# A Mamba-and-experts block on one Trainium2 core: order of the experts' products, the gate and a LayerNorm step inside a scan's slots

## The chip, the cores and the metric

The kernel runs on one core of one Trainium2 chip, as one launch. The metric is the device time of that core in microseconds, the median of three runs. A core has a matrix engine (PE, with its weight loads shown as PEld), a vector engine (DVE), an activation engine (ACT), a general engine (POOL) and a queue that starts the transfers (SP). Each works through its own list in order and waits on the others where the program says so.

## What is computed

The input is two images of 256 channels by 64x64 positions, read as two sequences of 4096 tokens. In short:

```python
x = x + conv_mamba(group_norm(x))                     # layer 0, inner width 256
t = tokens(x)
n = layer_norm(t)
t = t + mamba_fwd(ln(n)) + flip(mamba_bwd(flip(ln(n)))) + n   # layer 1, inner width 512 each
n = layer_norm(t)
w = softmax(mean_over_batch(n) @ Wr + br)             # 8 weights per token position
h = relu(bn(n @ W1[e]));  h = relu(bn(h @ W2[e]));  y_e = h @ Wo[e] + bo[e]
t = t + sum_e w[:, e] * y_e

# a mamba, for each channel d and state s (16 states), over time:
h = exp(dt * A[d, s]) * h + dt * B[s] * x
y[d] = sum_s C[s] * h[d, s] + D[d] * x;   out = (y * silu(z)) @ W_out
```

All of it is fp32.

## The kernel before

**The scan part.** Six Mamba jobs (batch 0: layer 0, forward, backward; then batch 1 the same) are each cut in 8 chunks of 512 tokens. A tile of 128 channels has 16 states, and the recurrence of 32 channels by 4 states fits 128 partitions, so a chunk is worked in groups of 4 x 512 columns: 640 groups `g` for the whole kernel, four to a tile of channels, eight to a pair of tiles (`n` is the place of the group among these eight). Each group is done in two halves `h`, each a *slot*; there are 1280 slots. One slot on each engine, in the order of the loop at the end of the scan part:

- PE: the products that a plan put in the slot (`pe`: input projections L434, convolution L472, dt L521, output L771 and L773, norms), then sums over states at some slots (`emit_sum`, L735, after the table `SUMS`), then the experts' products (`pe2`, L922).
- ACT: the copy of the last state (L724, L726), the two decays `exp(dt*A)` of the *next* slot (`emit_decay`, L684, with the join of L695), then whatever the plan put in `act`.
- DVE: what the plan put in `dve0` (convolution's second step L486 and the gate's sigmoid part L563), the scan (L705), what it put in `dve` (L533, the norms L399 and L400), then the multiplication by C (`emit_times_c`, L714). In three of eight groups (`POOL_C`) that last step is POOL's (L730), and the DVE's slot is then the scan alone.
- POOL: `b = x*dt*B` (L674), its share of the C products, `xdt` (L537) and the norm's residual add (L403).

The order on every engine is fixed by hand here (`in_order`). Work for later chunks is put into slots by fixed offsets relative to the chunk's first slot `s0` (`norm`, `prepare`, `finish`): for a layer-1 chunk the gate's projection z stands at s0-6, -5, -3 and -2 (`SLOTS`), with a load of ACT's function table at s0-6. Of the forward job's LayerNorm the divide (L399, L400) and POOL's add stand at s0-39, the affine step (L407, two activations) at s0-37, the store at s0-36. The add reads the tile `nx` that the affine step then overwrites. Since chunks are 32 slots apart, s0-38 of one chunk is s0-6 of the chunk ahead of it.

**The experts inside the scan part.** When the backward job has finished a chunk of tokens, the eight experts could be applied to it. `experts()` walks over the slots and adds groups of experts' products where a running balance of PE work (`behind`), of ACT work (`act_behind`) and the three PSUM banks of `psp` (`fits`) allow. One group is two matmuls of 128x512 for one half of one layer; a pair (one expert on one chunk of one batch) has six groups and leaves its result `u` in DRAM. At most one group goes into a slot. 68 of the 128 pairs are done this way: all 64 of batch 0, and experts 0 to 3 of chunk 7 of batch 1.

**The last part.** After the scans, `load`, `route` and `layer` go over the chunks 7, 6, ..., 0. For each expert not done early: L1162 twice with a ReLU (L1166), a multiplication by the routing weight (DVE, L1207) and L1212 into a PSUM accumulator of four banks (`ym`). For each pair done early, its `u` is loaded and added (`add_early`: DVE L1193 and L1197). At the end of a chunk the DVE reads the accumulator (L1224) before the next chunk's bias product (L1183) may write it. A chunk whose pairs are all early for both batches would be placed second (`whole`, `chunks[1:1]`); before the change there is none. A scheduler orders the instructions of this part.

Of the kernel before, what the change touches and what calls it, by code (L numbers as in the profile page):

```python
# [49 lines left out]
KC = C // P  # L50
# [30 lines left out]
PE_ROOM, PE_BEHIND = 3.8, 2.5  # L81
# [48 lines left out]
def hybrid_kernel(ctx: ExitStack, tc: tile.TileContext, a: dict, out: bass.AP):  # L130
# [75 lines left out]
    with ExitStack() as st:  # L206
# [129 lines left out]
        def norm(i):  # L336

            (job, c), ck, tag, s0 = steps[i], cks[i], tags[i], starts[i]
            s = job.cols(c)
            b = job.batch  # L340

            def alloc():
                ck["nx"] = wk.tile([P, KC, T], F32, tag="nx", name=f"nx_{tag}", bufs=2)

            if job.flip:
                def load():
                    alloc()
                    nc.sync.dma_start(ck["nx"], n2_dram[b][:, NCH - 1 - c, :, :])
                sl.put(s0 - 44, "sp", load)
                return  # L350

            def load_x():
                ck["x"] = wk.tile([P, KC, T], F32, tag="x", name=f"x_{tag}")
                src = t_dram[b] if job.layer else a["x"][b].rearrange("(k p) l -> p k l", p=P)
                nc.sync.dma_start(ck["x"], src[:, :, s])

            if job.layer == 0:
                def scale():
                    alloc()
                    for k in range(KC):  # L360
                        nc.scalar.activation(
                            ck["nx"][:, k, :], ck["x"][:, k, :], AF.Identity,
                            bias=job.gb[:, k : k + 1], scale=job.gs[:, k : k + 1],
                        )
                sl.put(s0 - 32, "sp", load_x)
                sl.put(s0 - 25, "act", scale)
                return

            def mean():
                ck["ps"] = psp.tile([P, T], F32, tag="ps", name=f"mean_{tag}")
                for k in range(KC):
                    nc.tensor.matmul(
                        ck["ps"], mean_w, ck["x"][:, k, :], start=(k == 0), stop=(k == KC - 1)
                    )

            def centre():
                ck["cen"] = wk.tile([P, KC, T], F32, tag="cen", name=f"cen_{tag}")
                nc.vector.tensor_tensor(ck["cen"], ck["x"], over_channels(ck["ps"]), ALU.subtract)  # L380

            def square():
                alloc()
                nc.scalar.activation(ck["nx"], ck["cen"], AF.Square)

            def variance():
                ck["var"] = psp.tile([P, T], F32, tag="ps", name=f"var_{tag}")
                for k in range(KC):
                    nc.tensor.matmul(
                        ck["var"], mean_w, ck["nx"][:, k, :], start=(k == 0), stop=(k == KC - 1)  # L390
                    )

            def roots():
                ck["r1"] = psp.tile([P, T], F32, tag="ps", name=f"r1_{tag}")
                rsqrt(ck["r1"], ck["var"], eps5)
                rsqrt(ck["var"], ck["var"], eps10, scale=1.0 + 1e-5)

            def divide():
                nc.vector.tensor_tensor(ck["nx"], ck["cen"], over_channels(ck["r1"]), ALU.mult)  # L399
                nc.vector.tensor_tensor(ck["cen"], ck["cen"], over_channels(ck["var"]), ALU.mult)  # L400

            def add():
                nc.gpsimd.tensor_tensor(ck["x"], ck["x"], ck["nx"], ALU.add)  # L403

            def affine():
                for k in range(KC):
                    nc.scalar.activation(  # L407
                        ck["nx"][:, k, :], ck["cen"][:, k, :], AF.Identity,
                        bias=lngb[:, 1, k : k + 1], scale=lngb[:, 0, k : k + 1],
                    )  # L410

            def store():
                nc.sync.dma_start(n2_dram[b][:, c, :, :], ck["nx"])
                nc.sync.dma_start(t_dram[b][:, :, s], ck["x"])

            for d, queue, fn in (
                (-48, "sp", load_x), (-44, "pe", mean), (-43, "dve", centre), (-42, "act", square),
                (-41, "pe", variance), (-40, "act", roots), (-39, "dve", divide), (-39, "pool", add),
                (-37, "act", affine), (-36, "sp", store),
            ):  # L420

                sl.put(s0 + d + (6 if c == 0 else 0), queue, fn)
            s0 += 6 if c == 0 else 0
            sl.count(s0 - 44, 2, 0, (1,))
            sl.count(s0 - 43, 0, 1)
            sl.count(s0 - 41, 2, 4, (2,))
            sl.count(s0 - 40, 0, 0, (1,))
            sl.count(s0 - 38, 0, 2)

        def in_proj(job, ck, half, j, name):  # L430
            ps = psp.tile([P, T], F32, tag="ps", name=name)
# [8 lines left out]
        def prepare(i):  # L440
# [109 lines left out]
            def gate(j):  # L550

                v = {}

                def pe():
                    v["ps"] = in_proj(job, ck, 1, j, f"z_{tag}_{j}")

                def act():
                    v["th"] = wk.tile([P, T], F32, tag="th", name=f"thz_{tag}_{j}", bufs=3)
                    nc.scalar.activation(v["th"], v["ps"], AF.Tanh, scale=0.5)

                def dve():
                    ck["sz", j] = wk.tile([P, T], F32, tag="sz", name=f"sz_{tag}_{j}", bufs=8)
                    nc.vector.scalar_tensor_tensor(  # L563
                        ck["sz", j], v["th"], 1.0, v["ps"], ALU.add, ALU.mult
                    )

                return (0, "pe", pe), (1, "act", act), (2, "dve0", dve)

            def put(slot, work):
                for d, queue, fn in work:  # L570
# [5 lines left out]
            for j in range(nj):  # L576
                put(at["xs"][j], xs(j))
                sl.count(s0 + at["xs"][j], 2, 1, (1,))
                put(at["dt"][j], softplus(j))
                sl.count(s0 + at["dt"][j], 1, 3, (2,))  # L580
                sl.count(s0 + at["z"][j], 2, 1, (1,))
            for jp in range(nj // 2):
                put(at["conv"][jp], conv(jp))
                sl.count(s0 + at["conv"][jp], 5, 1, (1, 2))
# [271 lines left out]
        def experts():  # L856
# [4 lines left out]
            def fits(slot):  # L861

                at = sum(b[0] <= slot for b in banks)
                both = banks[:at] + [(slot, slot + 1, 0)] + banks[at:]
                return all(
                    both[k - 3][1] + both[k][2] <= both[k][0] for k in range(max(3, at - 2), min(len(both), at + 4))
                    if at in range(k - 3, k + 1)
                )
# [9 lines left out]
            def follows(l):  # L878

                k, m = divmod(len(times[l]), KC)  # L880
                if k == len(todo):
                    return None
                waits = [(l - 1, k * KC + 1, 2)] if l else []
                if m:
                    waits.append((l, k * KC, 1))
                elif k:

                    waits.append((l, k * KC - 1, 6 if l == 0 and todo[k][-1] == 0 else 5))
                    if l < 2:
                        waits.append((l + 1, k * KC - 1, 0))  # L890
                if any(n >= len(times[w]) for w, n, _ in waits):
                    return None
                return max([todo[k][0] + 3] + [times[w][n] + d for w, n, d in waits])

            for slot in range(last):
                behind = max(0.0, behind) + sl.products.get(slot, 0) + sums_in(slot) - PE_ROOM
                act_behind = max(0.0, act_behind) + sl.acts.get(slot + 1, 0) - ACT_ROOM
                if behind + 2 > PE_BEHIND or act_behind + 1.3 > ACT_BEHIND or not fits(slot):
                    continue
                for l in (2, 1, 0):  # L900
                    at = follows(l)
                    if at is None or slot < at:
                        continue
                    banks.insert(sum(b[0] <= slot for b in banks), (slot, slot + 1, 0))
                    times[l].append(slot)
                    behind += 2
                    act_behind += 1 if l == 2 else 1.3
                    break
            put = [
                (*item[1:], [times[l][k * KC + m] for l in range(3) for m in range(KC)])  # L910
                for k, item in enumerate(todo) if (k + 1) * KC <= len(times[2])
# [109 lines left out]
        for g in range(nq):  # L1021
            i, jp, n = quads[g]
            for h in range(2):
# [3 lines left out]

                if (n, h) in ((1, 0), (5, 0)) and done:
                    emit_gate(*done.pop(0))

                if (n, h) in ((1, 1), (5, 1)):
                    emit_skip(i, 2 * jp + n // SG)
                sl.run(slot, "pe")
                for m in SUMS.get((n, h), ()):
                    if g - n + m >= 0:
                        emit_sum(g - n + m)
                sl.run(slot, "pe2")
                if (n, h) in ((0, 0), (4, 0)) and g:
                    done.append(at(g - 1)[:2])

# [292 lines left out]
```

## Time and profile before

| What | us |
|---|---|
| runs | 5367.55, 5373.43, 5375.16 |
| median | 5373.43 |
| profiled execution: its own time | 5375.72 |
| profiled execution: span from first to last instruction | 5373.7 |
| first scan starts, last scan ends | 61.1, 4567.2 |
| last part | 4571 to 5374 |
| busy in the span: PE, PEld, DVE, ACT, POOL | 4432.3, 1501.3, 4634.7, 3704.5, 4191.8 |

The profile shows one execution. A group row names line, engine, operation, out<-in and count, then busy time, the mean of one instruction in ns, the engine's idle time just before them and what ended it. A row of the waits says which line waited for which, for how long in total, how often, and the longest. In a timeline, the first column is the start, the second the duration of a merged run of equal instructions, and the bracket is the idle time ahead of it. A 128x512 fp32 matmul of the program stands in the trace as two records.

### The profile page before, as it was taken

To read this page: it belongs to the slowest core of one execution; us is meant where nothing else is said; L and a number is where in the kernel's file an instruction comes from. 1 tells how busy PE (TensorE), PEld (TensorE's weight loads), DVE (VectorE), ACT (ScalarE), POOL (GpSimd) and SP (SyncE) were. 2 spreads that over 40 slices of the span, in tenths; PEclk is the share of its full clock that TensorE was granted. 3 is DMA by queue.
4 is the path that set the end of the run, shared out by engine and by line. 5 is a ranking of instruction groups with operands and counts; after the bars stand their busy time and mean duration, and the time that the engine had idled before them with its cause. 6 is when DMAs were issued, how large, how long until landed. Compare 5 with 4: busy or idle time off the path is not lost.

```text
span 5373.7 us, 47307 instructions
## 1 busy us (share of the span) xinstructions
PE 4432.3 (82%) x14920; PEld 1501.3 (28%) x14920; DVE 4634.7 (86%) x3118; ACT 3704.5 (69%) x7722; POOL 4191.8 (78%) x1062
## 2 busy tenths in 40 slices
PE   5677777676678888889888888889898987699999
PEld 1122222221222333222222322223233332243433
DVE  6998999999999999989999999999999999423222
ACT  5677677777677777888887788887877787122222
POOL 6898999999999999988899999999999998000000
PEclk8888888888888999999999999999999999799999
DMA  4455333443345554455554445445544443623211
GB/s 170 145 176 172 137 126 129 154 149 133 128 142 185 170 165 152 167 191 191 193 184 160 165 173 177 164 166 169 192 160 161 157 165 126 235 74 113 95 63 47
DMA packets 307563, 822.41 MB, mean 153 GB/s; under 512 B 34472, under 2 KB 96688, under 8 KB 265328
## 3 DMA queue, kind: packets, MB, share of 16 engines
q1 hardware_dynamic: 307312, 819.39, 44.6%
q8 instruction: 118, 1.93, 0.1%
q14 instruction: 133, 1.09, 0.1%
HBM read 638.26 MB, written 181.01 MB: 152 GB/s over the span
## 4 chain that ended last, share of the span: by engine, by line
DVE 35%; PE 26%; ACT 12%; issue 7%; POOL 4%; DMA 3%; SPq 0%; DVEq 0%; POOLq 0%; ACTq 0%
DVE da L705 17%; PE hp L1162 7%; DVE bq L714 7%; DVE bq L705 6%; ACT da L684 4%; PE ym L1212 4%; PE e L922 4%; POOL bq L674 3%; PE y L735 3%; PE conv L472 2%; PE xs L434 2%; PE o L773 1%; POOL bq L730 1%; PE dbc L501 1%; DVE sz L563 1%
## 5 line engine op out<-in xcount | busy, mean ns | idle before, releaser
L674 POOL TENSOR_TENSOR bq<-rxdt,bc 128x2048 f32<-128x2048 f32 x640 | 2892.2, 4542 | 43.5 <-issue 22.3
L684 ACT ACTIVATE da<-rdt,w_a 128x512 f32<-128x512 f32 x2560 | 1756.6, 686 | 90.2 <-DVE bq L705 44.1
L705 DVE TENSOR_TENSOR_SCAN da<-da,h_state,bq 128x1024 f32<-128x1024 f32 x700 | 1644.2, 2349 | 16.9 <-issue 7.5
L730 POOL TENSOR_TENSOR bq<-bq,bc 128x2048 f32<-128x2048 f32 x240 | 1086.5, 4527 | 275.4 <-ACT h_state L726 261.7
L735 PE MATMUL y<-bq,stack 128*32 128x512 f32 x5120 | 835.1, 676 | 345.3 <-POOL bq L730 221.4
L714 DVE TENSOR_TENSOR bq<-da,bc 128x1024 f32<-128x1024 f32 x800 | 978.6, 1223 | 24.1
L705 DVE TENSOR_TENSOR_SCAN bq<-da,h_state,bq 128x1024 f32<-128x1024 f32 x420 | 965.5, 2335 | 24.7 <-ACT da L684 24.5
L724 ACT COPY h_state<-da 128x2 f32<-128x2 f32 x799 | 125.7, 157 | 770.1 <-DVE bq L714 768.8
L922 PE MATMUL e<-eh,ew 128*128 128x512 f32 x1088 | 552.2, 635 | 66.3 <-DVE sp L533 24.7
L1166 ACT ACTIVATE h<-hp,of,sc 128x512 f32<-128x512 f32 x240 | 186.5, 777 | 467.4 <-PE hp L1162 467.4
L1207 DVE TENSOR_TENSOR h<-h,wb 128x1024 f32<-128x1024 f32 x60 | 73.5, 1225 | 426.8 <-ACT h L1166 409.3
L695 ACT ACTIVATE bq<-h_state,bq,a 128x1 f32<-128x1 f32 x1120 | 432.2, 386 | 0.1
L735 PEld LDWEIGHTS y<-bq,stack 128*32 128x32 f32 x5120 | 150.4, 116 | 970.9 <-issue 367.5
L434 PE MATMUL z<-nx,w_in 128*128 128x512 f32 x640 | 326.3, 639 | 47.9 <-DVE sp L533 29.2
L434 PE MATMUL xs<-nx,w_in 128*128 128x512 f32 x640 | 334.5, 657 | 36.6 <-DVE xc L486 29.3
L472 PE MATMUL conv<-xs,w_conv 64*64 64x512 f32 x2560 | 330.2, 622 | 4.3 <-ACT eh L933 2.4
L922 PEld LDWEIGHTS e<-eh,ew 128*128 128x128 f32 x1088 | 198.4, 196 | 414.9 <-issue 230.6
L773 PE MATMUL o<-sz,w_out 128*128 128x512 f32 x640 | 303.5, 614 | 0.8 <-DVE sz L754 0.8
L922 PE MATMUL e<-en,ew 128*128 128x512 f32 x544 | 265.0, 614 | 22.3 <-DVE fcen L821 11.8
L521 PE MATMUL dt<-dbc,w_dt 64*128 64x512 f32 x320 | 200.9, 713 | 53.6 <-ACT dbc L508 32.3
L742 PE MATMUL y<-xc,w_d 128*128 128x512 f32 x320 | 185.3, 663 | 64.2 <-DVE sz L754 64.2
L1212 PE MATMUL ym<-h,Wo 128*128 128x512 f32 x480 | 231.8, 628 | 7.0 <-DVE h L1207 7.0
(139 smaller groups left out, 5178.5 us busy)
## 6 DMA issues: line engine op xcount, KB each, us to landing
rxdt<-xdtd SPq DMA_DIRECT2D x160, 1024.0 KB, 6.0
rdt<-dtd SPq DMA_DIRECT2D x160, 1024.0 KB, 5.8
bc<-bcd SPq DMA_DIRECT2D x384, 256.0 KB, 3.1
dtd<-sp SPq DMA_DIRECT2D x160, 256.0 KB, 3.8
xdtd<-xdt SPq DMA_DIRECT2D x160, 256.0 KB, 2.9
ew<-in_W SPq DMA_DIRECT2D x136, 256.0 KB, 4.0
u<-eu SPq DMA_DIRECT2D x68, 512.0 KB, 4.0
u<-u SPq DMA_DIRECT2D x68, 512.0 KB, 3.6
```

The costliest lines, as they stand in the source:

```text
L434: nc.tensor.matmul(ps, job.w["in", half][:, k, j * P : (j + 1) * P], rhs, start=(k == 0), stop=(k == KC - 1),)
L472: nc.tensor.matmul(v[r][64 * col : 64 * col + 64, :], job.w["conv"][rows, 2 * jp + j, k, :], ck["xs", jp][rows, j, k : k + T] if k < 4 els ...
L674: nc.gpsimd.tensor_tensor(bq[g], ck["rxdt", j], over_groups(ck["bc", 0, sg]), ALU.mult)
L684: nc.scalar.activation(da[g, h][:, k, :], cks[i]["rdt", j][:, q, :], AF.Exp, scale=steps[i][0].w["a"][:, j, q * SG + sg : q * SG + sg + 1],)
L695: nc.scalar.activation(bq[g][:, q, 0:1], job.h[:, j, sg, q : q + 1], AF.Identity, scale=cks[i]["a0", j][:, h, sg : sg + 1], bias=bq[g][:, ...
L705: nc.vector.tensor_tensor_scan(b if quads[g][2] in POOL_C else d, d, b, job.h[:, j, sg, 2 * h : 2 * h + 1] if c else 0.0, ALU.mult, ALU.add,)
L714: nc.vector.tensor_tensor(bq[g][:, two, :], d, cks[i]["bc", 1, sg].rearrange("p (o t) -> p o t", o=1).to_broadcast([P, 2, T]), ALU.mult,)
L730: nc.gpsimd.tensor_tensor(bq[g], bq[g], over_groups(cks[i]["bc", 1, sg]), ALU.mult)
L735: nc.tensor.matmul(y[i, j][q * CG : (q + 1) * CG, :], stack, bq[g][:, q, :], start=False, stop=(sg == SG - 1),)
L922: nc.tensor.matmul(ps, ew[l][:, k, m * P : (m + 1) * P], key[x][:, k, :], start=(k == 0), stop=(k == KC - 1),)
L1162: nc.tensor.matmul(ps, w[:, k, m * P : (m + 1) * P], x[:, k, :], start=(k == 0), stop=(k == KC - 1),)
L1212: nc.tensor.matmul(y[:, b, m, :], we["Wo", e][:, k, m * P : (m + 1) * P], h2[b][:, k, :], start=False, stop=(e == E - 1 and k == KC - 1),)
```

## The change

Five edits, all in how work is ordered:

1. `pe2` (experts' products) runs ahead of the sums over states in a slot, not behind them.
2. The planner of the experts may put two groups into a slot: it goes over the layers (2, 1, 1, 0, 0) and checks room before each; the second half of a layer may follow the first in the same slot (wait 0 in place of 1).
3. The gate's sigmoid part (L563) moves from the queue `dve0` to `dve`, from ahead of the scan to behind it, and the planner counts its PSUM bank for two slots.
4. The affine step of the LayerNorm moves from s0-37 to s0-38, and the plan's count of it with it.
5. With this the planner places 444 groups in 74 pairs, before 408 in 68. The six more are experts 4 to 7 of chunk 7 of batch 1 and experts 0 and 1 of chunk 6. Chunk 7 is then whole, so the last part runs the chunks 6, 7, 5, 4, ..., 0, with 6, 0, 8, 8, 8, 8, 8, 8 pairs of products. In the built program 66 slots hold two groups: 27 of them at place 15 of the 16 slots of a pair of tiles, 12 each at places 9 and 3, the other 15 elsewhere; 82 groups stand ahead of sums.

```diff
             for d, queue, fn in (
...
-                (-37, "act", affine), (-36, "sp", store),
+                (-38, "act", affine), (-36, "sp", store),
...
-            sl.count(s0 - 38, 0, 2)
+            sl.count(s0 - 39, 0, 2)
...
-                return (0, "pe", pe), (1, "act", act), (2, "dve0", dve)
+                return (0, "pe", pe), (1, "act", act), (2, "dve", dve)
...
-                sl.count(s0 + at["z"][j], 2, 1, (1,))
+                sl.count(s0 + at["z"][j], 2, 1, (2,))
...
                 if m:
-                    waits.append((l, k * KC, 1))
+                    waits.append((l, k * KC, 0))
...
-                if behind + 2 > PE_BEHIND or act_behind + 1.3 > ACT_BEHIND or not fits(slot):
-                    continue
-                for l in (2, 1, 0):
+                for l in (2, 1, 1, 0, 0):
                     at = follows(l)
                     if at is None or slot < at:
                         continue
+                    if behind + 2 > PE_BEHIND or act_behind + 1.3 > ACT_BEHIND or not fits(slot):
+                        break
                     banks.insert(sum(b[0] <= slot for b in banks), (slot, slot + 1, 0))
                     times[l].append(slot)
                     behind += 2
                     act_behind += 1 if l == 2 else 1.3
-                    break
...
                 sl.run(slot, "pe")
+                sl.run(slot, "pe2")
                 for m in SUMS.get((n, h), ()):
                     if g - n + m >= 0:
                         emit_sum(g - n + m)
-                sl.run(slot, "pe2")
```

## The prediction

> **What bounds the kernel now.** I read the page's busy rows and slices first, then a table of windows by stage, then the waits, then timelines at the places that the change touches. The busy rows, in tenths over 40 slices:
>
> ```profile
> PE   5677777676678888889888888889898987699999
> DVE  6998999999999999989999999999999999423222
> POOL 6898999999999999988899999999999998000000
> ```
>
> Up to slice 34 the DVE is full; after it the PE is and POOL is silent. The windows (us; then PE, PEld, DVE, ACT, POOL busy, clock, DMA) are cut where the first scan starts, where the experts begin (slot 447), and where the scans end:
>
> ```profile
> 61.00:1642.00 1581.00, 1114.75 (x4054) 328.04 (x4056) 1534.25 (x992) 1142.19 (x2453) 1479.25 (x376) 0.83 0.43 147
> 1642.00:4571.00 2929.00, 2550.79 (x9104) 861.73 (x9100) 2825.28 (x1830) 2334.28 (x4952) 2703.33 (x678) 0.95 0.49 169
> 4571.00:5374.00 803.00, 735.79 (x1644) 299.28 (x1644) 257.52 (x256) 204.46 (x271) 0.00 (x0) 0.94 0.31 105
> ```
>
> So two stages with two bounds: 4510 us in which the DVE is busy 4360 (97%), and 803 us in which the PE is busy 736 (92%). A pair moved from the second into the first is free as long as the DVE never waits for what it adds. The waits:
>
> ```profile
> ACT h_state L724 <- DVE bq L714: 768.8, 599, 17.4
> ...
> PE y L735 <- POOL bq L730: 221.4, 83, 11.4
> ...
> PE y L735 <- DVE bq L714: 123.0, 93, 3.5
> ...
> DVE sz L563 <- ACT thz L559: 35.6, 38, 4.1
> ...
> DVE bq L705 <- ACT da L684: 28.9, 25, 2.6
> ```
>
> ACT and the PE mostly wait for the DVE or POOL; the DVE's own waits are small, and the gate's (L563) is the largest.
>
> [...] the 221 us in which the PE stood before a sum are POOL's, with later products queued behind. [...] here L589 takes 1.28 us. [...] Here eight L1162 records took 5.28 us after an 18.5 us wait, against 3.60 warm.
>
> **Part 1, the last part: six pairs fewer.** A pair is 24 records; in steady state:
>
> ```profile
> 4705.91 3.60 PE L1212 MATMUL ym<-h,Wo 128*128 128x512 f32 x8
> 4709.35 1.02 PE L1162 MATMUL hp<-n,W 128*128 128x512 f32 x2
> 4710.20 3.87 PE L1162 MATMUL hp<-h,W 128*128 128x512 f32 x8
> 4713.92 2.74 PE L1162 MATMUL hp<-n,W 128*128 128x512 f32 x6
> 4716.49 3.60 PE L1212 MATMUL ym<-h,Wo 128*128 128x512 f32 x8
> ```
>
> From one L1212 to the next is 10.58 us; six pairs are 63.5. But the order of chunks changes, so I lay out the start. In the old trace, scans' end to the bias product of chunk 5 is 4571 to 4785.7, 214.7 us: a first routing until 4597.5 (loads), four pairs of chunk 7 with an 18.5 us stall at 4643 (the routing of the next chunk sits on the DVE behind 12 early adds), then chunk 6, 100 us. New, in the built order: routing again to 4597.5; products of pairs 2, 3, 4 of chunk 6, a bias and a routing product, 41 us, to 4638. The DVE, free to start at 4614.6 (routing weights landed), has some 18 operations of 1.17 us and small ones ahead of that routing: about 4641, so 3 us of stall, not 18.5. Pairs 5, 6, 7 and a routing product: 31.7 + 3.7 + 2 for the cold clock, to 4679. Chunk 7 has no products to lay over its adds: until the DVE has done the four outputs of chunk 6 (4 x 1.17), ten more operations and the small ones, about 17 us, the PE has only the bias (3.7) and stands some 14 us; then 8 us of chunk 5's first products: its bias at about 4707. Old 4785.7, new 4707: **-78 us**. The 16 added `u` loads of this chunk (median 3.6 us to landing, four buffers) lie beside 39 us of DVE adds. If they or the routing weights land late, 10 to 15 us go; if the stall is hidden, 10 come. Ends: -62 to -88.
>
> **Part 2, the gate behind the scan.** L563's waits inside the scan stage sum to 33.7 us: 4 are of 2.4 to 4.1, the others up to 1.2, most of them at place 12 of the 16 slots of a pair of tiles. Behind a scan of 2.35 us only the excess of the four long ones is left, some 4 us: -29.7. The bank is held one scan longer: PE's o (L771) waits for it in layer 0, and then its sums run 2.2 us later; the gate that reads them mostly had 3.2 us to spare there, so nothing. Of the 33.7, 6.3 us lie at the places of part 3 and are counted there: **-23 us**.
>
> **Part 3, the affine step one slot earlier.** This is where I expect a new wait. Around slot 890, ACT:
>
> ```profile
> 3223.90 1.41 ACT L684 ACTIVATE da<-rdt,w_a 128x512 f32<-128x512 f32 x2
> 3225.32 1.28 ACT L589 ACT_TABLE_LOAD   x1
> ...
> 3227.39 1.41 ACT L684 ACTIVATE da<-rdt,w_a 128x512 f32<-128x512 f32 x2
> 3228.73 0.58 ACT L559 ACTIVATE thz<-z 128x512 f32<-128x512 f32 x1
> 3229.21 1.51 ACT L407 ACTIVATE nx<-cen,lngb 128x512 f32<-128x512 f32 x2
> ```
>
> POOL, whose add reads the tile that L407 overwrites, and the DVE:
>
> ```profile
> 3225.70 2.36 POOL L403 TENSOR_TENSOR x<-x,nx 128x1024 f32<-128x1024 f32 x1
> ```
>
> ```profile
> 3224.03 4.58 DVE L705 TENSOR_TENSOR_SCAN bq<-da,h_state,bq 128x1024 f32<-128x1024 f32 x2
> 3229.34 0.69 DVE L563 SCALAR_TENSOR_TENSOR sz<-thz,z 128x512 f32<-128x512 f32 x1 [0.73 <-ACT thz L559]
> ```
>
> In the built program L407 now follows the table load and precedes the decays at 3227.39. POOL ends at 3228.1, so ACT stands until then, runs 1.51 us, then join and decays: ready at 3231.1. The scans before end at 3228.6: the DVE waits 2.5 us where it had waited 0.7. Queued behind L407 are exactly those decays; the DVE waits for them, POOL and the PE for the DVE. This place is two scan-only slots in a row, so nothing covers it. The same reading of all 16 LayerNorm chunks (add's end against the end of ACT's slot): 12 wait for POOL, the other four only pay the 1.51 us; the stalls sum to 31.6 us, against 6.3: **+25 us**. Cover could come only from POOL being earlier, and it runs without a gap into the add. Ends: 0 and +32.
>
> **Part 4, more experts' work.** Six pairs add 36 groups: 36 x 4 records x 0.43 = 62 us of PE in a stage where it idles 378 of 2929; 24 ReLUs of 0.77 and 12 copies of 0.58 = 25 us of ACT, which idles 595; 18 weight loads and 6 stores on SP's queue, DMA at 0.49. Sums over 2929 us fit; what counts is the slot. ACT's fixed work there is 0.39 + 1.41 and a copy, about 2.0 us of 3.5, or of 2.35 where the DVE's slot is the scan alone. Of the 66 doubled slots, 24 (places 9 and 3) put two activations (1.54) into the first of two such short slots: 2.0 + 1.5 + 1.8 = 5.3 us against two scans, 4.7. That is 0.6 us each, **+14 us**; at place 15 (27 slots) a gate's DVE operation of 0.68 in that slot hides it. Ends: 0, and a whole activation pair for all 66, +102.
>
> **Part 5, products ahead of sums.** 82 groups of 1.72 us now stand before sums. Their reader on the DVE is the gate L754 two slots on: wherever the new plan puts such a group, 36 gates, the old trace shows 2.6 us or more between last sum and gate. POOL's buffers (6) come free two groups before they are needed, and POOL waited 8 us in all for it. Gain: the PE no longer stands with products behind a sum; the DVE's waits on late PE results are some 20 us in this stage. I take **0**, ends -10 and +10.
>
> **Sum.** -78 - 23 + 25 + 14 + 0 = -62 on the span of 5373.7; the profiled execution (5375.72) has 2 us around the span, and is 2.3 above the median of 5373.4. From the median: 5311 us.
>
> **Rivals.**
> - *The affine wait and the doubled slots are covered* (POOL's add earlier, ACT ahead): 5373 - 78 - 23 = 5272. For it: ACT idles 770 us on L724. Against: the timeline, where no idle lies ahead of those decays.
> - *ACT's clumps cost more*: another 30 us of waits at L705, 5341. For: 25 such waits exist already. Against: the planner's balance for ACT.
> - *The whole chunk does not pay*: with no products of its own, late `u` loads stretch it; the last part gains only 45: 5344.
> - *Slower*: the second group in a slot makes the decays late by its activation pair each time. The gain without part 4 is 76 us; 66 slots turn it round from 1.15 us each; at a whole pair, 1.54, it is +102: 5399. Against: part 4's count, and 1.5 us of lead that ACT has in ordinary slots.
> - That the change does not do what it says: the built program holds the 74 pairs, so no.
>
> **Chances.** Forecast (scan stage 0 to +30, last part -70 to -85) 0.52; covered 0.19; clumps 0.13; chunk does not pay 0.08; slower 0.05; rest 0.03. The forecast's own range is 5290 to 5325. The range reaches to the covered case and to most of the clumps: 5272 to 5341. A measurement of this kernel tells 0.2%, about 11 us, from no change. All cases but the slower one, and half of the rest, are faster by more: 0.93; within 0.02; slower 0.05.
>
> **What would show it.** Right: the last part at about 725 us, with one PE stall of 10 to 17 us in the second chunk; L563's waits below 8 us; a new wait of ACT L407 on POOL L403, 10 to 15 times, and L705 waiting for L684 by some 25 to 50 us more; the scans' end at 4570 to 4595. Wrong: no wait at L407, L754 waiting for the PE by over 20 us, POOL waiting for L735, or the last part above 745.

## The result and the profile after

The changed kernel takes 5341.66 us (median of 5 runs, 5337.19 to 5343.66) beside 5368.28 for the kernel before (median of 5, 5366.43 to 5375.16; the three runs ahead of the forecast had 5373.43): ratio 0.9947, 95% interval 0.9935 to 0.9958, 27 us less. The forecast was 5311 with a range from 5272 to 5341. Its profiled execution has 5339.88 us, span 5338.1. Line numbers of the scan part are unchanged up to L773; the experts' products are L921 now (before L922), and lines of the last part are 2 lower.

The busy rows of the changed kernel, in tenths over 40 slices:

```profile
PE   5677777777667888888878888888998888789999
DVE  6999999999999999998989999999999999663222
POOL 6898999999999998988989999999999999400000
```

The shape is that of before: the DVE is full until the scans end, now inside slice 34 (counted from 0), where POOL still works too. The windows of the changed kernel, cut at the same three events (us; then PE, PEld, DVE, ACT, POOL busy, clock, DMA):

```profile
60.00:1656.00 1596.00, 1128.30 (x4052) 334.40 (x4052) 1529.11 (x992) 1141.51 (x2454) 1479.37 (x376) 0.82 0.42 146
1656.00:4612.00 2956.00, 2561.49 (x9244) 883.54 (x9244) 2815.19 (x1828) 2355.76 (x4989) 2704.48 (x678) 0.95 0.50 170
4612.00:5338.00 726.00, 670.50 (x1506) 271.93 (x1504) 266.40 (x264) 185.80 (x247) 0.00 (x0) 0.94 0.35 120
```

The last part fell from 806.5 us (4567.2 to 5373.7) to 725.6 (4612.5 to 5338.1): -81. The scan stage, from the first scan's start to the last one's end, grew from 4506.1 to 4552.2: +46, some 14 of them already where no experts are. The forecast had +16. The waits of the changed kernel that stand against those shown of before:

```profile
ACT h_state L724 <- DVE bq L714: 736.1, 579, 17.4
...
PE y L735 <- POOL bq L730: 152.7, 59, 11.4
...
DVE da L705 <- ACT da L684: 60.0, 44, 3.1
...
PE e L921 <- DVE sz L563: 56.5, 37, 3.4
...
DVE sz L754 <- PE y L735: 47.8, 39, 4.0
...
DVE bq L705 <- ACT da L684: 29.6, 24, 2.2
```

and, from the same view filtered by engine:

```profile
DVE sz L563 <- ACT thz L559: 2.4, 2, 1.2
...
ACT nx L407 <- POOL x L403: 18.4, 12, 1.9
```

Of the kernel before, three rows more of the same view:

```profile
DVE sz L754 <- PE y L735: 12.9, 19, 2.4
...
PE e L922 <- DVE sz L563: 8.3, 3, 5.0
...
DVE da L705 <- ACT da L684: 7.9, 11, 1.3
```

This is a trade. L563 waited 35.6 us for the gate's tanh and waits 2.4 (twice, ahead of the first scan). L407's wait on POOL is new, 12 times, and the scan's wait for its decays (L705 on L684, both forms) rose from 36.8 to 89.6. The PE stood 69 us less for POOL ahead of a sum, yet L754, which reads the sums, waits 47.8 us where it waited 12.9: the PE now stands 56.5 us ahead of experts' products for L563 (8.3 before).

Where the affine step lies, ACT in the changed kernel (start, duration, idle ahead in the bracket), near the place that the prediction read:

```profile
3256.55 1.41 ACT L684 ACTIVATE da<-rdt,w_a 128x512 f32<-128x512 f32 x2
3257.98 1.28 ACT L589 ACT_TABLE_LOAD   x1
3261.16 1.52 ACT L407 ACTIVATE nx<-cen,lngb 128x512 f32<-128x512 f32 x2 [1.90 <-POOL x L403]
3262.58 0.37 ACT L695 ACTIVATE bq<-h_state,bq,a 128x1 f32<-128x1 f32 x1
3262.86 1.40 ACT L684 ACTIVATE da<-rdt,w_a 128x512 f32<-128x512 f32 x2
```

and the DVE there:

```profile
3256.69 4.58 DVE L705 TENSOR_TENSOR_SCAN bq<-da,h_state,bq 128x1024 f32<-128x1024 f32 x2
3264.34 2.36 DVE L705 TENSOR_TENSOR_SCAN da<-da,h_state,bq 128x1024 f32<-128x1024 f32 x1 [3.07 <-ACT da L684]
```

ACT stands for POOL's add, then does the affine step, then the decays; the scan waits 3.07 us. All 7734 records of ACT in this trace, as all 7722 in that of before, start in the order of the program; so the decays behind L407 come after its 1.90 us of wait and its 1.52. At the places that follow the LayerNorm chunks' affine steps the scans wait some 34 us in all (31.6 were forecast).

Where a sum comes late, PE in the changed kernel:

```profile
3724.09 1.98 PE L921 MATMUL e<-en,ew 128*128 128x512 f32 x4
3728.00 2.68 PE L921 MATMUL e<-eh,ew 128*128 128x512 f32 x4 [1.92 <-DVE sz L563]
3730.61 1.94 PE L735 MATMUL y<-bq,stack 128*32 128x512 f32 x8
```

and the DVE:

```profile
3725.08 2.28 DVE L705 TENSOR_TENSOR_SCAN bq<-da,bq 128x1024 f32<-128x1024 f32 x1
3727.28 0.66 DVE L563 SCALAR_TENSOR_TENSOR sz<-thz,z 128x512 f32<-128x512 f32 x1
3727.86 2.28 DVE L705 TENSOR_TENSOR_SCAN bq<-da,bq 128x1024 f32<-128x1024 f32 x1
3732.61 0.69 DVE L754 SCALAR_TENSOR_TENSOR sz<-y,sz 128x512 f32<-128x512 f32 x1 [2.47 <-PE y L735]
```

L563 ends at 3727.94 and the group of experts starts at 3728.00: it waited for the PSUM bank of z, which L563 reads only after its scan. The sums stand behind that group, and L754 behind the sums: 1.92 us of wait and 2.68 of group. So two parts of the change meet here: the gate behind the scan and the products ahead of the sums.

The last part, PE in the changed kernel, at its second chunk:

```profile
4725.15 6.48 PE L1181 MATMUL ym<-wts,bo 8*128 8x512 f32 x8 [0.40 <-DVE o L1222]
4740.15 1.02 PE L1123 MATMUL wt<-ident,w 128*8 128x128 f32 x4 [8.53 <-DVE w L1118]
4740.96 4.57 PE L1160 MATMUL hp<-n,W 128*128 128x512 f32 x8
4745.37 3.87 PE L1160 MATMUL hp<-h,W 128*128 128x512 f32 x8
4749.17 3.69 PE L1181 MATMUL ym<-wts,bo 8*128 8x512 f32 x8
```

The PE stands 8.53 us once in the chunk that has no products, and its records around it are long (6.48 against 3.69 for the same bias product): the granted clock was 0.55 over the 6.48 us, 0.50 over the 8.53, 0.79 over the 4.57 and 1.00 over the 3.69. In the kernel before it was 0.56 over the stall of 18.54 us, 0.68 over the 5.28 us of eight L1162 records behind it and 1.00 over the 3.60 us of the same eight at 4597.54; the 2 us that part 1 took for the cold clock are the difference of these two, 1.68. Chunk 5's bias starts at 4749.2, 136.7 us after the scans' end; the forecast laid it out as 136 (4571 to 4707).

### The profile page after: what moved, and what is told of

Its sections match the earlier page's. It is cut to its first block, busy times and chain, and to the rows that moved or that the text cites. A ratio compares the mean times of both kernels' runs of the same rounds, so it can differ in the third digit from the quotient of the medians.

```text
span 5338.1 us, 47443 instructions
## 1 busy us (share of the span) xinstructions
PE 4391.2 (82%) x14920; PEld 1502.0 (28%) x14920; DVE 4628.4 (87%) x3124; ACT 3706.4 (69%) x7734; POOL 4192.4 (79%) x1062
## 4 chain that ended last, share of the span: by engine, by line
DVE 43%; PE 29%; ACT 14%; issue 8%; POOL 4%; DMA 3%; SPq 0%; DVEq 0%; POOLq 0%; ACTq 0%
DVE da L705 22%; DVE bq L714 10%; PE hp L1160 7%; DVE bq L705 6%; ACT da L684 6%; PE e L921 5%; PE ym L1210 3%; PE conv L472 3%; PE y L735 3%; PE xs L434 2%; POOL bq L674 2%; PE o L773 2%; ACT bq L695 1%; DVE xc L486 1%; ACT sp L530 1%
## 5 line engine op out<-in xcount | busy, mean ns | idle before, releaser
L684 ACT ACTIVATE da<-rdt,w_a 128x512 f32<-128x512 f32 x2560 | 1756.5, 686 | 84.1 <-DVE bq L705 38.3
L705 DVE TENSOR_TENSOR_SCAN da<-da,h_state,bq 128x1024 f32<-128x1024 f32 x700 | 1644.2, 2349 | 64.9 <-ACT da L684 55.2
L714 DVE TENSOR_TENSOR bq<-da,bc 128x1024 f32<-128x1024 f32 x800 | 976.6, 1221 | 19.8
L705 DVE TENSOR_TENSOR_SCAN bq<-da,h_state,bq 128x1024 f32<-128x1024 f32 x420 | 967.6, 2335 | 23.0 <-ACT da L684 23.0
L735 PE MATMUL y<-bq,stack 128*32 128x512 f32 x5120 | 774.6, 668 | 218.7 <-POOL bq L730 152.7
L921 PE MATMUL e<-eh,ew 128*128 128x512 f32 x1184 | 590.8, 627 | 98.2 <-DVE sz L563 29.2
L1164 ACT ACTIVATE h<-hp,of,sc 128x512 f32<-128x512 f32 x216 | 167.8, 777 | 420.1 <-PE hp L1160 414.6
L434 PE MATMUL z<-nx,w_in 128*128 128x512 f32 x640 | 342.4, 662 | 78.8 <-DVE sp L533 39.2
L921 PE MATMUL e<-en,ew 128*128 128x512 f32 x592 | 307.0, 653 | 85.4 <-DVE fcen L821 34.5
L735 PEld LDWEIGHTS y<-bq,stack 128*32 128x32 f32 x5120 | 144.3, 116 | 795.7 <-issue 382.8
L434 PE MATMUL xs<-nx,w_in 128*128 128x512 f32 x640 | 325.0, 638 | 41.3 <-DVE xc L486 23.8
L921 PEld LDWEIGHTS e<-eh,ew 128*128 128x128 f32 x1184 | 215.4, 194 | 458.3 <-issue 192.8
L773 PE MATMUL o<-sz,w_out 128*128 128x512 f32 x640 | 304.1, 615 | 0.8 <-DVE sz L754 0.8
L932 ACT ACTIVATE eh<-e,of,sc 128x512 f32<-128x512 f32 x296 | 224.3, 769 | 30.9 <-PE e L921 30.2
L537 POOL TENSOR_TENSOR xdt<-sp,xc 128x512 f32<-128x512 f32 x160 | 203.4, 1274 | 45.1 <-DVE sp L533 45.1
```

The costliest lines, as they stand in the source:

```text
L434: nc.tensor.matmul(ps, job.w["in", half][:, k, j * P : (j + 1) * P], rhs, start=(k == 0), stop=(k == KC - 1),)
L684: nc.scalar.activation(da[g, h][:, k, :], cks[i]["rdt", j][:, q, :], AF.Exp, scale=steps[i][0].w["a"][:, j, q * SG + sg : q * SG + sg + 1],)
L705: nc.vector.tensor_tensor_scan(b if quads[g][2] in POOL_C else d, d, b, job.h[:, j, sg, 2 * h : 2 * h + 1] if c else 0.0, ALU.mult, ALU.add,)
L714: nc.vector.tensor_tensor(bq[g][:, two, :], d, cks[i]["bc", 1, sg].rearrange("p (o t) -> p o t", o=1).to_broadcast([P, 2, T]), ALU.mult,)
L735: nc.tensor.matmul(y[i, j][q * CG : (q + 1) * CG, :], stack, bq[g][:, q, :], start=False, stop=(sg == SG - 1),)
L773: nc.tensor.matmul(v[m], job.w["out"][:, j, m * P : (m + 1) * P], ck["sz", j], start=False, stop=(j == job.nj - 1),)
```

## The experiments

All edits are of the changed kernel unless said otherwise. The ratio is to the kernel before, run on the same chip. "Scan stage" is first scan's start to last scan's end in the profiled execution; the waits are the totals of the waits view, in us (some 22 us of L486's lie ahead of the first scan in every run). The sets e1 to e4, e5 to e8, f1 to f3 and g1 ran on four chips, on which the kernel before took 5372.0, 5369.0, 5375.2 and 5368.7 us. So a difference of medians between two sets is good to some 7 us only; the scan stages stand beside it below, and each of these is of one execution, which no run repeats.

| Run | median us | ratio (95%) | scan stage | L705 on L684 | L754 on L735 | L563 on L559 | L486 on L481 |
|---|---|---|---|---|---|---|---|
| before | 5368 to 5375 | 1 | 4506.1 | 36.8 | 12.9 | 35.6 | 35.5 |
| changed | 5341.66 | 0.9947 (0.9935 to 0.9958) | 4552.2 | 89.6 | 47.8 | 2.4 | 40.4 |
| e1_affine | 5314.69 | 0.9894 (0.9879 to 0.9909) | 4520.5 | 50.6 | 46.5 | 2.4 | 43.4 |
| e2_gate | 5338.69 | 0.9941 (0.9929 to 0.9954) | 4548.9 | 35.5 | 16.1 | 84.8 | 27.5 |
| e3_sums | 5322.20 | 0.9907 (0.9894 to 0.9921) | 4527.3 | 87.7 | 28.1 | 2.4 | 37.5 |
| e4_gate_sums | 5337.37 | 0.9936 (0.9923 to 0.9948) | 4550.2 | 38.3 | 15.6 | 79.0 | 30.7 |
| e5_gate_alone | 5364.16 | 0.9989 (0.9982 to 0.9995) | 4495.6 | 42.1 | 34.4 | 2.4 | 48.9 |
| e6_one_group | 5382.06 | 1.0021 (1.0013 to 1.0029) | 4515.7 | 70.1 | 32.0 | 2.4 | 45.1 |
| e7_affine_sums | 5284.84 | 0.9841 (0.9828 to 0.9855) | 4494.4 | 53.5 | 25.3 | 2.4 | 41.4 |
| e8_no_nine | 5274.00 | 0.9823 (0.9809 to 0.9836) | 4486.3 | 48.3 | 25.2 | 2.4 | 41.2 |
| f1_gate_layer | 5270.91 | 0.9808 (0.9794 to 0.9821) | 4480.3 | 44.4 | 14.4 | 19.1 | 32.3 |
| f2_gate_ahead | 5297.89 | 0.9858 (0.9845 to 0.9872) | 4507.3 | 39.8 | 14.0 | 33.7 | 33.9 |
| f3_plan_alone | 5304.24 | 0.9870 (0.9856 to 0.9883) | 4512.9 | 37.3 | 15.1 | 41.3 | 30.7 |
| g1_gate_counted | 5355.20 | 0.9975 (0.9966 to 0.9984) | 4495.2 | 40.2 | 31.1 | 2.4 | 51.1 |

Theory "the bank", drawn from the profile above: of the 30 us that the scan stage grew beyond the forecast, most come from products that wait for the bank of z ahead of sums. Rival, "the order alone": groups ahead of sums make them late whenever the bank comes free.

**e1_affine: the affine step back by one slot.**

```diff
-                (-38, "act", affine), (-36, "sp", store),
+                (-37, "act", affine), (-36, "sp", store),
```

> The changed kernel with the affine step L407 back at s0-37; the plan of products is untouched. In the changed kernel L407 stood 12 times on POOL's L403, 18.4 us, and the scans at place 12 that follow the 16 LayerNorm chunks waited 34.5 us for their decays. If that step makes those waits: L407 waits for POOL no more, L705's waits for L684 fall by 30 us or more (from 89 to about 57), and the kernel needs 28 to 34 us less, about 5311. If ACT is late there anyway because of the second group in a slot: the wait moves to another scan, and less than 12 us is gained.

27.0 us less. L407 waits for POOL no more, and L705's waits for its decays fell by 39.0; the scan stage is 31.7 us shorter. Shown: the early affine step makes the wait that part 3 laid out. POOL waiting for `b` tiles and L486 took a few us of it back.

**e2_gate, e3_sums, e4_gate_sums: gate and order, each alone and both.**

```diff
# e2_gate and e4_gate_sums
-                return (0, "pe", pe), (1, "act", act), (2, "dve", dve)
+                return (0, "pe", pe), (1, "act", act), (2, "dve0", dve)
# e3_sums and e4_gate_sums
-                sl.run(slot, "pe2")
                 for m in SUMS.get((n, h), ()):
                     if g - n + m >= 0:
                         emit_sum(g - n + m)
+                sl.run(slot, "pe2")
```

> The changed kernel with the gate's sigmoid part L563 back ahead of the scan (dve0); the plan, the order of products and sums, and the affine step are untouched. Theory 'the bank': the PE's next product (o L771, or a group of the experts, e L921) waits for the bank of z until L563 has read it, one scan of 2.35 us longer than before, and the sums stand behind that product; so L754's waits for sums fall from 46 us to under 18, L563's waits of some 30 us return, and the kernel comes out within 15 us of the changed one (5335 to 5357). Theory 'the order alone': the sums are late because groups of experts stand ahead of them, whenever the bank comes free; then L754 keeps 35 us or more in the stage with experts and the kernel needs 25 to 45 us more, 5367 or above.

> The changed kernel with the sums over states ahead of the experts' products in a slot again; the rest is untouched. Theory 'the bank': only groups of experts that wait for the bank of z can hold the sums in the stage with experts; behind the sums they do no harm, so of L754's 29.8 us there 8 or less remain; the 16 us of the stage without experts stay, since there o L771 waits, which stands ahead of the sums in both orders. Time 15 to 25 us less than the changed kernel. Rival 'the order pays elsewhere': products behind a sum wait for POOL or the DVE, their results reach ACT late, and L705 waits more: nothing gained, or 10 us and more lost.

> The changed kernel with both: L563 ahead of the scan, and the sums ahead of the experts' products. Theory 'the bank': either one alone already takes the waits of L754 in the stage with experts, so the two gains don't add: L754 at 10 to 15 us in all as in the kernel before, L563 some 30 us, time within 8 us of the run with L563 alone ahead of the scan. Theory 'the order alone': here and with the sums alone the waits fall, with L563 alone they don't; then this run is 25 us or more below that one.

With the gate behind the scan, products ahead of sums cost 19.5 us (5341.66 against 5322.20; 24.9 of scan stage); with the gate ahead of it, 1.3 (5338.69 against 5337.37; the scan stage is 1.3 shorter). So neither part makes the sums late by itself; together they do. The order alone is refuted. e1 and e7, with the affine step back in both, repeat the first of the two: 26.1 us of scan stage. In e3_sums the PE, at the place shown above:

```profile
3712.98 1.88 PE L921 MATMUL e<-en,ew 128*128 128x512 f32 x4
3714.79 1.07 PE L735 MATMUL y<-bq,stack 128*32 128x512 f32 x8
3715.79 1.99 PE L921 MATMUL e<-eh,ew 128*128 128x512 f32 x4
```

and the DVE:

```profile
3714.66 0.66 DVE L563 SCALAR_TENSOR_TENSOR sz<-thz,z 128x512 f32<-128x512 f32 x1
3715.24 2.28 DVE L705 TENSOR_TENSOR_SCAN bq<-da,bq 128x1024 f32<-128x1024 f32 x1
3717.44 0.67 DVE L754 SCALAR_TENSOR_TENSOR sz<-y,sz 128x512 f32<-128x512 f32 x1
```

The sum starts before L563 ends, the group for that bank runs behind it, and L754 follows its scan without a gap. The two runs with the gate ahead show one thing more: there L563 waits some 80 us, not 35, since ACT's stall behind L407 now ends at the gate, which stands ahead of the scan (with the affine step back, in f3, it waits 41.3). One rival stays: such waits of the DVE give the PE time, and might hide late sums in e2. The places speak against it: in the changed kernel 25.4 of L754's 47.8 us lie at place 2 of the 16 slots, and 8.1 are left there in e2, while L563's waits in e2 lie at places 8 to 12. No run has gate ahead, products ahead and the affine step back.

**e5_gate_alone: the kernel before with the gate behind the scan, nothing else.** The same line as in e2_gate, from `dve0` to `dve`, in the kernel before.

> The kernel before with one edit: the gate's sigmoid part L563 behind the scan; plan, order and affine step as before. The sums stand ahead of the experts' products here, so only o L771 of layer 0 can hold them while it waits for the bank of z. Theory 'the bank': L563's 33.7 us of waits go to 0 and the DVE's records overlap 13 us more as in the changed kernel, L754's waits grow by about 12 us, nearly all at place 10 of layer-0 chunks: 30 to 38 us less than before, about 5338. The rival, that the wait for the gate's tanh passes on to the sums or the decays: less than 12 us gained.

A miss: 4.9 us less in the median and 10.5 in the scan stage, not 30 to 38. The DVE's records do fill 15.5 us less (4357.8 to 4342.3), as the last section tells; the waits don't. The DVE's waits in this run:

```profile
DVE xc L486 <- ACT thx L481: 48.9, 23, 14.4
DVE sz L754 <- PE y L735: 34.4, 29, 3.9
...
DVE da L705 <- ACT da L684: 14.1, 27, 1.9
```

L563's 33.2 us are gone, and L754 has 21.5 more, L486 13.4, L705 5.3, which is 40.2: the wait changed its place and grew. What L754 gained lies at place 10 of layer-0 chunks, where o L771 waits for the bank of z ahead of the sums; L486 had not been thought of. The rival of this run held.

**e6_one_group: no second group in a slot.**

```diff
                 for l in (2, 1, 1, 0, 0):
+                    if slot in times[0] + times[1] + times[2]:
+                        break
```

> The changed kernel with at most one group of experts in a slot; order, gate and affine step as changed. The planner then places 67 pairs, one fewer than before, and no chunk is whole for both batches. If the second group in a slot is what lets 74 pairs in and costs little: the last part takes 806 + 11 = 817 us, the scans end some 20 us earlier than in the changed kernel (the 17 us of L705's waits at place 12 that lie at no LayerNorm chunk go), and the whole takes some 5410. If the doubled slots cost the scans far more than L705 shows: the scans end 40 us and more earlier, and the whole is below 5390.

67 pairs, 5382.06 us where 5410 were expected. The last part took 803.3 us (817 expected; it differs little from the 806.5 with 68 pairs), and the scans ended 36.5 us sooner in the stage, more than the 20 that L705 accounted for: L754 fell by 15.8 too, probably as fewer groups stand ahead of sums. So doubled slots, and the seven pairs that they let in, were worth 40 us net in the changed kernel, 77.7 won in the last part and 36.5 paid in the scan stage.

**e7_affine_sums: affine step and order of sums both put back.** The edits of e1_affine and e3_sums together.

> The changed kernel with the affine step at s0-37 and the sums ahead of the experts' products. If the two waits (decays behind L407, sums behind a product that waits for its bank) are separate, the gains of the two runs add: 27 + 19.5 less than 5341.7, 5295. If ACT or the PE is late anyway once one of them is gone, less than 35 us are gained: above 5307.

56.8 us less than the changed kernel. On the scan stage it is 57.8, beside 31.7 and 24.9 of the two alone: the waits are separate, and the gains add. (By medians it is 10 more than the sum, across two chips.)

**e8_no_nine: e7_affine_sums, and no second group at place 9.**

```diff
                 for l in (2, 1, 1, 0, 0):
+                    if slot % 16 == 9 and slot in times[0] + times[1] + times[2]:
+                        break
```

> As the run with both put back, and the planner puts no second group into place 9 of a pair of tiles; it still places 74 pairs (54 doubled slots, none at place 9, 12 at place 3). If the two ReLUs of such a slot, with the table load beside them, make the scan at place 12 late: of the 13 us that L705 waits there without the affine step, 3 or less remain, and the time falls by 8 to 14 us against that run, to about 5284. If ACT's work as such is too much: the waits come back at other places and the time is the same within 4 us.

10.8 us less (8.1 of scan stage). L705's waits for decays at place 12 fell from 13.6 us to 5.8, not to 3, and nothing came back elsewhere (L754 and L486 stayed): the two ReLUs beside the table load made most of them.

**f1_gate_layer, f2_gate_ahead, f3_plan_alone: what the gate is worth without the harm.** The first two edit e8_no_nine, the third e7_affine_sums.

```diff
# f1_gate_layer
+                return (0, "pe", pe), (1, "act", act), (2, "dve" if nj == 4 else "dve0", dve)
# f2_gate_ahead and f3_plan_alone
+                return (0, "pe", pe), (1, "act", act), (2, "dve0", dve)
```

> As the run without second groups at place 9 (5274.0), with the gate's L563 back ahead of the scan in the chunks of layer 0 alone, where o L771 needs the bank of z one slot after the gate; in layer 1 it stays behind the scan. If the bank is what makes the sums of layer 0 late: L754's waits fall from 23 us to about 11, L486's by some 5, L563 waits 6 to 10 us again and the DVE's records overlap 3 us less: 3 to 8 us less in all, about 5269. If the waits only change their place: 5274 within 3, or more.

> As the run without second groups at place 9 (5274.0), with L563 back ahead of the scan in all chunks. In the kernel before, the move by itself brought 5 us; with the affine step at s0-38 and the sums first, 15 us (5337.4 against 5322.2). If the 15 contained the stall behind L407, which an operation ahead of the scan takes in full, this run is 3 to 8 us above 5274; if the move is worth 15 us where the sums stand ahead of the products, 5286 to 5292.

> The planner's edit alone: the plan of 74 pairs with up to two groups in a slot, while affine step, gate and order of sums and products are as in the kernel before (the changed kernel with these three put back). From 5284.8 of the run with affine step and sums put back, the gate's move is 5 us (as alone in the kernel before) or 15 (as with the affine step early): 5290 or 5300. Either way 69 us or more below the kernel before. If the doubled slots need the gate behind the scan: above 5310.

f2 lies 23.9 us above e8 and f3 19.4 above e7, on another chip; by the ratios it is 19 and 16, by the scan stages 21.0 and 18.5. So the gate's move is worth 16 to 24 us on this plan, as much as the higher of the values I had expected (15) or more. f1 is 3.1 us below e8; its interval overlaps that of e8, though its scan stage is 6.0 shorter. Its waits answer to the theory (L754 -10.8, L486 -8.9, L563 +16.7):

```profile
DVE sz L563 <- ACT thz L559: 19.1, 13, 4.1
DVE sz L754 <- PE y L735: 14.4, 21, 3.1
```

f1 has the lowest time of all, 1.9% below the kernel before and about 70 us below the changed one. Its windows:

```profile
61.00:1633.00 1572.00, 1105.86 (x4052) 325.45 (x4052) 1528.61 (x991) 1141.84 (x2452) 1478.98 (x376) 0.83 0.43 148
1633.00:4542.00 2909.00, 2554.73 (x9244) 879.43 (x9244) 2817.29 (x1829) 2354.34 (x4989) 2704.23 (x678) 0.96 0.51 173
4542.00:5269.00 727.00, 669.78 (x1504) 271.80 (x1504) 265.76 (x263) 185.80 (x247) 0.00 (x0) 0.95 0.35 120
```

The last part is that of the changed kernel; with six pairs more in it, the scan stage is still 26 us shorter than before.

**g1_gate_counted: why the gate alone brought so little.** The kernel before, with the edit of e5_gate_alone and

```diff
-                sl.count(s0 + at["z"][j], 2, 1, (1,))
+                sl.count(s0 + at["z"][j], 2, 1, (2,))
```

> The kernel before with L563 behind the scan, as in the run with the gate alone, and in addition the planner's count of z's bank for two slots, as the changed kernel has it; 67 pairs in place of 68. In the run with the gate alone the plan still took the bank as free after one slot. If that is why the move brought 5 us there and 19 on the plan of 74 pairs: the experts' products wait less for L563, L754's and L486's waits fall from 34.4 and 48.9 us to about 25 and 41, and the scan stage is 18 us or more below the 4506.1 of before. If the count makes no difference, because one group in a slot is what puts the groups there: both waits stay within 4 us and the scan stage stays at 4490 to 4498.

The scan stage is that of e5 within 0.4 us, L754 and L486 within 3.3: the count is not the reason. The median is 13.5 us below the kernel before, though a pair fewer is placed, and the profiled spans of both runs are alike (5358.8 and 5359.4); so the gate's move alone is worth 5 to 13 us, 10.5 by the scan stage.

## Why the prediction was right and wrong

The runs build the change up part by part: plan alone (f3), then the gate (e7), then the early affine step (e3), then products ahead of sums (the changed kernel). Each term of the forecast's sum beside the step of the scan stage that it stands for (one execution each):

| Term | forecast | measured | from |
|---|---|---|---|
| 1, last part | -78 | -81 | 806.5 to 725.6 |
| 4, doubled slots | +14 | +6.8 | before to f3 |
| 2, gate | -23 | -18.5 | f3 to e7 |
| 3, affine step | +25 | +32.9 | e7 to e3 |
| 5, products ahead of sums | 0 | +24.9 | e3 to changed |
| sum, on spans | -62 | -35.6 | 5373.7 to 5338.1 (0.8 of it ahead of the first scan) |

The medians differ by 27 and not 36, since the profiled execution of before lies 7 us above its median of five, and that of the changed kernel 2 below: the sum took 2.3 for this.

The step that failed is part 5: "I take **0**, ends -10 and +10". It cost 24.9 us of scan stage and 19.5 of the median, beyond the upper end. The argument was that each such gate had 2.6 us or more between last sum and gate, and a group is 1.72 us. It priced the group and left out what the group itself waits for. Part 2 had just said that the bank of z is held one scan longer and then followed only o L771 with it, "so nothing"; the three banks are shared, and the next to ask for one was in more than half of the cases a group of experts (37 of the PE's 70 waits for L563 in the changed kernel), which part 5 had moved ahead of the sums. At the place shown, 2.68 us of group and 1.92 of wait are more than 2.6. Such waits do little harm where no sum stands behind them: in e7, with the sums ahead, the PE waits 53.0 us for L563 ahead of experts' products, in the changed kernel 56.5, but L754 waits 25.3 in place of 47.8.

The two parts were costed one by one, and the 2x2 of e2, e3 and e4 shows that the cost lies in their meeting. Taken in the other order the same loss falls to part 2: with the products already ahead of the sums (e2 to the changed kernel), the gate's move makes the scan stage 3.3 us longer. The list of what would show the forecast wrong named the sign, "L754 waiting for the PE by over 20 us", and gave no such case a chance. The rival "ACT's clumps cost more" named 5341, about the time measured, but mostly not for its reason: L705's waits for decays rose by 52.8 us, and some 34 of these are the affine step's.

Part 3 was right in mechanism and count (12 waits on POOL, as laid out). Its size on the scan stage is 31.7 us where it is taken out of the changed kernel and 32.9 where it is added to e7. The forecast's +25 is 31.6 less the 6.3 that the gate's tanh already cost at these places. In the build-up the gate moves first, so the 6.3 belong to its step: like for like it is +31.6 against +32.9 here and -29.7 against -18.5 for the gate. In the changed kernel each of the 96 table loads of L589 took 1283 ns, and ACT's next record followed a load by 12 ns in the median of 116, so a load needed no further price.

Part 1 was right to 3 us, though the PE's stall was 8.5 us and not 14, with slower records behind it in its place. Part 4's +14 for places 9 and 3 is +6.8 on the stage, and the 12 slots at place 9 are 5.6 of it (f3 to f2; 8.1 from e7 to e8): those at place 3, where no table load stands, cost nothing that shows.

Part 2 named the right waits and had the wrong account of what becomes of them; that its size came out near (-18.5 for -23) is luck. From f3 to e7, L563's waits fall by 38.9 us, and those of L705, L486 and L754 rise by 16.2, 10.7 and 10.2, which is 37.1. So the waits changed their place, and the gain is nearly all in the DVE's records, which fill 15.0 us less (4358.6 to 4343.6); of this the forecast knew nothing. On the plan before, the records fill 15.5 us less, and the waits cost more than L563 gave, so the move is worth 5 to 13 us. Why the waits grow less on the new plan (in e7 L754 waits 25.3 us and L486 41.4, in e5 34.4 and 48.9) is open: the groups of experts lie in other slots there; the bank's count is ruled out, and no run moved single groups.

## What to carry to other kernels

When a reader of a buffer is moved back, look for everyone who asks for a buffer of that pool next, other edits' arrivals among them, and then for what is queued behind it. A piece of work costs its duration and its own waits (2.68 and 1.92 us at the place shown), and parts of a change that touch the same pool must be priced together. And a wait that is taken from one place of a full engine is a gain only when the next work is ready: here 33 to 39 us of L563's waits came back at other lines, nearly all or more than all.

## What was not expected of the hardware

The DVE's time in the scan stage, the union of its records, is 4357.8 to 4359.4 us in the runs with the gate ahead of the scan and 4342.0 to 4345.0 with it behind: the same 2819 records fill 13 to 17 us less. (f1, with the gate ahead in layer 0 alone, has 4345.9.) The changed kernel's DVE shows it:

```profile
1764.14 2.35 DVE L705 TENSOR_TENSOR_SCAN da<-da,h_state,bq 128x1024 f32<-128x1024 f32 x1
1766.52 1.23 DVE L714 TENSOR_TENSOR bq<-da,bc 128x1024 f32<-128x1024 f32 x1
1767.66 2.35 DVE L705 TENSOR_TENSOR_SCAN da<-da,h_state,bq 128x1024 f32<-128x1024 f32 x1
1769.92 0.67 DVE L563 SCALAR_TENSOR_TENSOR sz<-thz,z 128x512 f32<-128x512 f32 x1
1770.51 1.21 DVE L714 TENSOR_TENSOR bq<-da,bc 128x1024 f32<-128x1024 f32 x1
```

L714 directly behind the scan whose output it reads starts 0.03 us after that scan's end (1766.49). With the gate between them, L563 starts 0.09 before the scan's end (1770.01) and L714 0.08 before L563's (1770.59). The pair of a scan and its L714 without idle time stands 698 times in the kernel before and 574 times in the changed one: 124 times some 0.12 us is 14.5 us, of which 4.2 lie between the records and 10.3 belong to the 13 to 17; where the rest lies was not followed. In these records an operation that reads its predecessor's result starts about 0.12 us later than one that doesn't. Small operations show it too: L316 and L317, or L849 and L850, which read the result just ahead of them, start 0.035 us after its end, while L714 behind L400, whose result it does not read, starts 0.08 before. Whether the data make it or the wait of the DVE for itself that the program sets there, no run took apart.
